# Four graph layers on one core: mixes by tiles, statistics ahead of evictions, and a few moved instructions

## The chip, the cores and the metric

The kernel runs on one core of one Trainium2 chip. The metric is the device time in microseconds (us), the median of three runs. A profiled execution of the same kernel gives the trace that is read here.

## The reference, cut to what matters

The input x holds 128 graphs of 64 nodes with 256 features each; adj is one 64 by 64 matrix for all graphs. Everything is in fp32. Each of four layers normalises x over its features, takes the positive part, runs its own network and adds the result to x.

```python
h = relu(layernorm(x)); x = x + L0(h)      # the same for L1, L2, L3
# L0: two graph convolutions, then LSTM windows of length 1 to 4 over the nodes
h = relu(einsum('ts,bsh->bth', adj, x @ Wg0 + bg0))
h = relu(einsum('ts,bsh->bth', adj, h @ Wg1 + bg1))
for p in 1..4: h[last node of each window of p] = lstm_last(Wih[p-1], Whh[p-1], windows of p)
# L1: masked attention with 4 heads
# L2: A_hat = normalised (adj + I)
h = relu(batchnorm(einsum('nm,bmd->bnd', A_hat, x) @ W1.T + b1)); out = batchnorm(h @ W2.T + b2)
# L3: weighting = adj * adj
h = relu(weighting . (x @ W1)); h = relu(weighting . (h @ W2)); out = weighting . (h @ W3)
```

## The kernel before, in words

The 8192 rows of x are cut into NG = 16 groups of 512 rows. A group is a tile of 128 partitions by GT = 4 row tiles by 256 features, so that a row tile holds two graphs. Most of x stays in SBUF from layer 1 on. Each layer runs over the groups, and the work of neighbouring groups overlaps.

**Mix.** A product with the 64 by 64 matrix of a layer is called a mix (the helper `mix`, matmuls on line 133). For each pair of column chunks it takes two PSUM banks and fills them with matmuls of 64 by 64: a loop over the two chunks c outermost, then over the four row tiles t, then over two column halves and the two graphs. In fp32 each of these matmuls is two instructions of TensorE, so that one pair of chunks is 64 instructions. Two copies then bring the banks to SBUF (lines 142, 145 and 381), one of them per graph, on the engines named in `copies`.

**Layer norm.** `ln_scale` takes statistics on VectorE (lines 90 and 92), adds epsilon (93), takes the power -1/2 on GpSimd (94) and multiplies on VectorE (96). `ln_apply` then runs one ScalarE activation for each row tile (101).

**Layer 0, convolutions.** The loop takes for each step `first_mix(g)`, `second_weights(g - 2)` (matmuls on 430), `second_mix` and `first_weights(g)` (matmuls on 406, an addition of `rb0` on VectorE in 414, a maximum on GpSimd in 415). The bias `rb0` is scaled by the row sums on line 346, behind group 1's place in VectorE's order. At group 4 the small forms of the adjacency are made, `normalized_adjacency` among them: 13 small VectorE instructions, one GpSimd power (326), a transpose on TensorE (280, four instructions), and a last product on VectorE (330). Its result `ah2` is used in layer 2 alone. The x of later groups is loaded into three buffers, and a load waits for the `ln_apply` that frees its buffer.

**Layer 0, LSTM, and layer 3's dense products** use a seven-product scheme for 2 by 2 blocks (helper `seven`): four products go first, then partial sums, then three more products, with the results added and finished by the callback `end`. The matmuls of the LSTM are on line 484, those of layer 3 on 1028, 1064 and 1109.

**Layer 1** is attention, with its projection weights in `w_att`. **Layer 2** makes `activated(g + 1)` and `mixed(g + 1)` ahead of `hidden(g)`. `hidden` runs sixteen matmul instructions (703) into four banks, and for each bank a ScalarE eviction with bias (709) and then VectorE statistics (712). The batch norm is finished after the last group (`bn_finish`), and a second loop runs the second weights (957). Its two weights come in one go at the end of layer 1, into a tile that follows `w_att`.

**Layer 3**: `start` (residual, layer norm, mix), `first_weights` (1028), `second_mix` (133, copies 142), `second_weights` (1064), `third_weights` (1109), `last_mix` (1130). In `first_weights` the last block (1, 0) of 128 by 512 is added on VectorE (176) and cut at zero on VectorE (204); the other blocks are cut on ScalarE (202, 206).

**Order.** Each engine runs its instructions in one fixed order, which the framework plans when the kernel is built: mostly as the program has it, but instructions that could start earlier are moved forward by the planner's costs. `tc.issue_after(ins)` puts the instructions of its block behind `ins` on the engine of `ins` only. Reading one PSUM bank from two engines is ordered too, in the order of the program. DMAs go out in the order of the issuing queue, here mostly that of SyncE (SP).

Of the kernel before, what the change touches and what calls it, by code (L numbers as in the profile page):

```python
# [10 lines left out]
ALU = mybir.AluOpType  # L11
# [3 lines left out]
P = 128  # L15
# [23 lines left out]
def adj_preln_kernel(ctx: ExitStack, tc: tile.TileContext, x_in, adj, vec, bg0, bg1,  # L39
# [42 lines left out]
    def ln_scale(src, between=None, n=GT):  # L82
# [10 lines left out]
        nc.vector.tensor_scalar(rstd, mv[:, :, 1], LN_EPS, None, ALU.add)  # L93
# [3 lines left out]
        return rstd, nmr, last.ins  # L97

    def ln_apply(src, dst, rstd, nmr, n=GT):
        for t in range(n):  # L100
            nc.scalar.activation(  # L101
                dst[:, t, :], src[:, t, :], AF.Relu,
                bias=nmr[:, t : t + 1], scale=rstd[:, t : t + 1],
            )

    def ln_relu(src, dst):

        rstd, nmr, _ = ln_scale(src)
        ln_apply(src, dst, rstd, nmr)
# [11 lines left out]
    def mix(src, a2, chunks, dst, copies, swap=False):  # L121
# [3 lines left out]
        for c0 in range(0, chunks, 2):  # L125
            pss = [bank((P, 2, GT, NODES)) for _ in range(2)]
            for c in range(2):
                for t in range(GT):
# [23 lines left out]
    def seven(products, banks, p1, p5, out, end):  # L152
# [14 lines left out]
        def finish():  # L167
# [8 lines left out]
            nc.vector.tensor_tensor(out[1][0], p1, ps[3], ALU.add)  # L176
            end(1, 0, None)
# [18 lines left out]
    def ends_in(out, func, on_vector=()):  # L196

        def end(m, n, ps):  # L200
            if ps is not None:
                nc.scalar.activation(out[m][n], ps, func)
            elif (m, n) in on_vector:
                nc.vector.tensor_scalar(out[m][n], out[m][n], 0.0, None, ALU.max)
            elif func != AF.Copy:
                nc.scalar.activation(out[m][n], out[m][n], func)  # L206

        return end
# [45 lines left out]
    with tc.tile_pool(name="lw", bufs=5) as lw:  # L254
# [6 lines left out]
        with tc.tile_pool(name="gw", bufs=1) as gw, tc.tile_pool(name="gcn", bufs=2) as gp, \  # L261
# [48 lines left out]
            def normalized_adjacency():  # L310
# [17 lines left out]
                pt2 = bank((P, NODES))  # L328
                by_batch(pt2, an)
                nc.vector.tensor_scalar(ah2, pt2, dinv, None, ALU.mult)  # L330
# [13 lines left out]
            with tc.issue_after(first_ln):  # L344
                nc.vector.tensor_reduce(rsum, arow, AX.X, ALU.add)
                nc.vector.tensor_scalar(rb0[:, 0, :], rb0[:, 0, :], rsum, None, ALU.mult)
# [4 lines left out]
            first_copied, first_scalar, middle_copied = None, None, None  # L351

            def first_mix(g):
                nonlocal first_copied, middle_copied, first_scalar
                h = gp.tile([P, GT, D], F32, tag="h", name="h")
                if g == 0:
                    for k, (rstd, nmr, _) in enumerate(lns):
                        two = slice(2 * k, 2 * k + 2)
                        ln_apply(xs[0][:, two], h[:, two], rstd, nmr, 2)
                elif g == 1:  # L360
                    with tc.issue_after(first_ln):
# [14 lines left out]
                if g == 0:  # L376
# [9 lines left out]
                    first_copied = copied  # L386
                else:
                    copied = mix(h, adj2, 2, m0, (on_vector, on_vector))
                if g == NG // 4:

                    with tc.issue_after(copied):
                        adjacency_forms()
                        normalized_adjacency()
                if g == NG // 2:
                    middle_copied = copied
                return m0
# [54 lines left out]
        with tc.tile_pool(name="back", bufs=1, reuse_waits="tile") as back_pool, \  # L451
# [22 lines left out]
            def gate_set(p, n, g, gates, w, bs):  # L474
# [25 lines left out]
                def end(m, blk, ps):  # L500
# [186 lines left out]
    def activated(pool, g):  # L687

        a = arena(pool)
        ln_relu(xs[g], a[:, 0:2, :].rearrange("p a (b d) -> p (a b) d", d=D))  # L690
# [6 lines left out]
    def hidden(g, w1, ms=range(4)):  # L697
        a = h1s[g]
        pss = []
# [8 lines left out]
        for m, ps in zip(ms, pss):  # L708
            nc.scalar.activation(
                a[:, m, :], ps, AF.Identity, bias=vecs[:, V_B1 + m : V_B1 + m + 1]  # L710
            )
            last = nc.vector.bn_stats(st1[:, m, g, :], ps)  # L712
        return last.ins


    with tc.tile_pool(name="att", bufs=2, reuse_waits="tile") as ap_:
# [113 lines left out]
        for g in range(NG + 1):  # L830
# [8 lines left out]
            if g == NG:  # L839

                w_l2 = weight_tile()
                w1 = w_l2[:, 0]
                w2 = w_l2[:, 1].rearrange("p (c f) -> p c f", c=4)
                w1 = w1.rearrange("p (c f) -> p c f", c=2)
                nc.sync.dma_start(out=w1, in_=w1t.rearrange("(c p) f -> p c f", p=P))
                nc.sync.dma_start(out=w2, in_=w2t.rearrange("(c p) f -> p c f", p=P))
# [3 lines left out]
            if g < NG:  # L850
                q, k = queries_keys(hT)
                v = ap_.tile([P, 2 * GT, P], F32, tag="v", name="v")
# [54 lines left out]
    behind = [after_attention, after_attention, counted]  # L907
    for g in range(1, NG):
        if g + 1 < NG:
            with tc.issue_after(behind[g - 1]):  # L910
                pool = ar_right if g + 1 < NG // 2 else keep if g + 1 == NG // 2 else ar_left
                activated(pool, g + 1)
                mixed(g + 1, (on_vector, on_vector))
# [336 lines left out]
```

## Time and profile before

| what | value |
|---|---|
| median of 3 runs | 2531.91 us (2531.35 to 2533.04) |
| profiled execution | 2532.12 us, its span 2530.3 us |
| TensorE busy | 2478.1 us, 98% of the span; mean granted clock 0.994 |
| VectorE, ScalarE, GpSimd busy | 1469.4, 1119.3, 419.4 us |
| chain that ended last | PE 90%, DVE 5%, ACT 2%, issue 1%, POOL 1%, DMA 1% |
| DMA | 39.64 MB, mean 16 GB/s |
| instruction fetch, queue 8 | 158 packets, 2.59 MB |

The span runs from the first to the last instruction; 1.8 us of the execution lie around it. In the profile PE is TensorE, PEld its weight loads, DVE VectorE, ACT ScalarE, POOL GpSimd and SP SyncE. A line of the timeline gives start, length, engine, line of the kernel, operation, tiles, shapes and count, and in brackets the idle time before it with what ended it. By the chain, the convolutions of layer 0 take the time up to 186 us, the LSTM up to 1232, attention up to about 1478, layer 2 up to about 1733, and layer 3 the rest.

### The profile page before, as it was taken

Reading aid. Unit: us, or ns where it says so; the run is one execution under the profiler, and the core shown is the slowest. Engines: PE = TensorE matmul, PEld = TensorE weight load, DVE = VectorE, ACT = ScalarE, POOL = GpSimd, SP = SyncE. Lnnn points to the kernel's source line nnn. Section 1 sums busy time; section 2 is a strip of 40 time slices with the busy share of each in tenths; the row PEclk is TensorE's granted clock in tenths of the full one; section 3 lists DMA queues with packets and bytes.
Section 4 is the critical chain, followed back from the end, with each engine's and each line's share of the span. In section 5 each row is a group of like instructions: output and inputs, shape, how many; then the busy total and the mean of one; then the engine's idle time right before and its main releaser. Section 6 shows DMA issues by size and latency. Waiting matters only on the chain.

```text
span 2530.3 us, 46856 instructions
## 1 busy us (share of the span) xinstructions
PE 2478.1 (98%) x20190; PEld 2044.8 (81%) x20190; DVE 1469.4 (58%) x2626; ACT 1119.3 (44%) x1967; POOL 419.4 (17%) x352
## 2 busy tenths in 40 slices
PE   6999999999999999999999999998999999999999
PEld 4668888889999998888766654445898888888888
DVE  5648876666566565565566666515455554554544
ACT  3547764444455343444455454653333332332332
POOL 3322211111111111111122221003111111111110
PEclk9999999999999999999999999998999999999999
DMA  3200000000000000000300000010000000000000
GB/s 112 102 2 1 1 17 1 1 1 34 1 1 1 1 1 1 1 13 1 101 2 2 2 19 1 1 48 12 9 10 10 18 10 9 18 10 9 18 9 18
DMA packets 30079, 39.64 MB, mean 16 GB/s; under 512 B 1584, under 2 KB 26288, under 8 KB 29872
## 3 DMA queue, kind: packets, MB, share of 16 engines
q1 hardware_dynamic: 29168, 36.09, 4.3%
q8 instruction: 158, 2.59, 0.4%
q10 hardware_dynamic: 704, 0.56, 0.1%
q14 instruction: 49, 0.40, 0.1%
HBM read 28.26 MB, written 8.39 MB: 14 GB/s over the span
## 4 chain that ended last, share of the span: by engine, by line
PE 90%; DVE 5%; ACT 2%; issue 1%; POOL 1%; DMA 1%; POOLq 0%; DVEq 0%; ACTq 0%
PE ps L484 40%; PE ps L1064 15%; PE ps L1109 8%; PE ps L731 4%; PE ps L957 4%; PE ps L1028 4%; PE ps L133 3%; PE ps L747 2%; PE ps L406 2%; PE ps L430 2%; DVE st L90 1%; POOL rstd L94 1%; PE ps L703 1%; ACT arena L101 1%; DVE st L712 1%
## 5 line engine op out<-in xcount | busy, mean ns | idle before, releaser
L484 PE MATMUL ps<-diff,s 128*128 128x256 f32 (+1 forms) x1824 | 393.5, 371 | 0.9 <-DVE diff L600 0.9
L1064 PE MATMUL ps<-arena 128*128 128x256 f32 x1792 | 392.6, 381 | 1.1 <-DVE arena L185 1.1
L1064 PEld LDWEIGHTS ps<-arena 128*128 128x128 f32 x1792 | 337.8, 190 | 55.3 <-issue 10.7
L484 PEld LDWEIGHTS ps<-diff,s 128*128 128x128 f32 x1824 | 345.9, 190 | 33.8 <-issue 1.6
L498 ACT ACTIVATE gates<-gates,lbias 128x512 f32<-128x512 f32 (+5 forms) x426 | 244.2, 621 | 203.6 <-DVE gates L173 146.5
L168 POOL TENSOR_TENSOR gates<-p 128x512 f32<-128x512 f32 (+1 forms) x115 | 148.6, 1292 | 882.8 <-DVE p L165 831.7
L484 PE MATMUL ps<-h,w 128*128 128x256 f32 (+1 forms) x1028 | 241.2, 371 | 1.6 <-ACT p L161 1.6
L484 PE MATMUL ps<-diff,w 128*128 128x256 f32 (+1 forms) x1040 | 238.7, 370 | 0.0
L484 PEld LDWEIGHTS ps<-diff,w 128*128 128x128 f32 x1040 | 197.4, 190 | 18.2
L484 PEld LDWEIGHTS ps<-h,w 128*128 128x128 f32 x1028 | 194.6, 190 | 20.9 <-ACT p L161 2.0
L498 ACT ACTIVATE gates<-ps,lbias 128x256 f32<-128x256 f32 (+3 forms) x213 | 91.7, 476 | 247.1 <-PE ps L484 247.0
L206 ACT ACTIVATE arena<-arena 128x512 f32<-128x512 f32 x128 | 78.7, 628 | 192.7 <-POOL arena L168 104.0
L168 POOL TENSOR_TENSOR arena<-arena 128x512 f32<-128x512 f32 x64 | 73.4, 1146 | 537.0 <-DVE arena L165 537.0
L1109 PE MATMUL ps<-arena 128*128 128x128 f32 x1280 | 149.9, 276 | 0.0
L1109 PEld LDWEIGHTS ps<-arena 128*128 128x128 f32 x1280 | 145.6, 192 | 1.3 <-issue 0.2
L173 DVE TENSOR_TENSOR gates<-p,ps 128x512 f32<-128x512 f32 (+1 forms) x115 | 76.4, 664 | 120.2 <-PE ps L484 120.2
L173 DVE TENSOR_TENSOR arena<-arena,ps 128x512 f32<-128x512 f32 x64 | 39.7, 621 | 149.1 <-PE ps L1064 84.3
L94 POOL TENSOR_TENSOR rstd<-rstd,mhalf 128x4 f32<-128x4 f32 (+1 forms) x66 | 66.7, 1010 | 338.5 <-DVE rstd L93 327.4
L703 PE MATMUL ps<-arena,w 128*128 128x512 f32 x256 | 115.2, 603 | 4.7 <-DVE arena L145 4.7
L484 PE MATMUL ps<-state,w 128*128 128x256 f32 (+1 forms) x512 | 116.1, 370 | 0.9 <-ACT p L161 0.8
L101 ACT ACTIVATE arena<-x,nmr,rstd 128x256 f32<-128x256 f32 x128 | 67.7, 590 | 109.8 <-DVE nmr L96 104.4
L484 PE MATMUL ps<-state,s 128*128 128x256 f32 (+1 forms) x512 | 115.8, 369 | 0.0
(186 smaller groups left out, 3934.5 us busy)
## 6 DMA issues: line engine op xcount, KB each, us to landing
x<-in_x SPq DMA_DIRECT2D x27, 512.0 KB, 7.6
out<-x SPq DMA_DIRECT2D x15, 512.0 KB, 2.9
w<-in_wih SPq DMA_DIRECT2D x4, 1024.0 KB, 7.3
w<-in_whh SPq DMA_DIRECT2D x3, 1024.0 KB, 6.2
arena<-in_l3w SPq DMA_DIRECT2D x3, 1024.0 KB, 5.2
w<-in_wqkv SPq DMA_DIRECT2D x1, 768.0 KB, 4.3
x<-in_x SPq DMA_DIRECT2D x2, 256.0 KB, 3.0
wg<-in_wg ACTq DMA_DIRECT2D x2, 256.0 KB, 7.2
```

Of the source, the lines that this page charges most:

```text
L94: nc.gpsimd.tensor_tensor(out=rstd, in0=rstd, in1=mhalf[:, 0:n], op=ALU.pow)
L101: nc.scalar.activation(dst[:, t, :], src[:, t, :], AF.Relu, bias=nmr[:, t : t + 1], scale=rstd[:, t : t + 1],)
L168: nc.gpsimd.tensor_tensor(out=out[1][1], in0=p1, in1=p5, op=ALU.add)
L173: nc.vector.tensor_tensor(out[0][1], p1, ps[1], ALU.add)
L484: nc.tensor.matmul(ps[:, r], lhsT=wc[:, j, :], rhs=bc, start=first and r == 0 and c == 0, stop=True, skip_group_check=True,)
L498: nc.scalar.activation(o, ps, func, bias=lbias[:, col : col + 1])
L703: nc.tensor.matmul(ps, lhsT=w1[:, c, m * P : (m + 1) * P], rhs=a[:, 2 + c, :], start=(c == 0), stop=(c == 1),)
L731: nc.tensor.matmul(ps, lhsT=wqk[:, c, col : col + P], rhs=hT[:, c, :], start=(c == 0), stop=(c == 1),)
L957: nc.tensor.matmul(pss[m], lhsT=w2[:, c, m * P : (m + 1) * P], rhs=a[:, c, :], start=(c == 0), stop=(c == 3),)
L1028: nc.tensor.matmul(ps[:, t, :], lhsT=w[:, t * P : (t + 1) * P], rhs=b, start=first and t == 0, stop=True, skip_group_check=True,)
L1064: nc.tensor.matmul(ps[:, r, :], lhsT=w[:, c, col : col + P], rhs=b[:, c, :], start=first and r == 0 and c == 0, stop=c == 1, skip_group_ch ...
L1109: nc.tensor.matmul(ps[:, t, :], lhsT=w[:, c, t * P : (t + 1) * P], rhs=b[:, c, :], start=first and t == 0 and c == 0, stop=c == 3, skip_gr ...
```

## The change

The changed kernel computes the same. It differs in these places:

- `mix` has the loop over row tiles t outermost and the one over chunks c inside it.
- In the first group of layers 0 and 3, the normalisation of row tile 3 moves from ScalarE (one instruction) to VectorE (two instructions). In layer 3's first group, the second half of the residual and its statistics come behind line 93 of the first half.
- The scaling of `rb0` and group 1's layer norm in layer 0 come behind the first group's copies on VectorE.
- The transpose on line 280 of the normalised adjacency and the product behind it come at group 8; the rest stays at group 4.
- In layer 2, statistics come ahead of evictions in the program; line 96 of group g + 1 comes behind the second statistics of group g - 2; one copy of each mix moves from VectorE to ScalarE.
- The first weights of layer 2 are loaded into the columns of `w_att` that the last queries and keys leave free, in the last step of attention; the second weights follow in two parts at group 3 of layer 2's loop in the program.
- Block (1, 0) of layer 3's first weights is added in two parts, one for each row tile, each cut at zero on ScalarE.

```diff
-        nc.vector.tensor_scalar(rstd, mv[:, :, 1], LN_EPS, None, ALU.add)
+        var = nc.vector.tensor_scalar(rstd, mv[:, :, 1], LN_EPS, None, ALU.add)
...
-        return rstd, nmr, last.ins
+        return rstd, nmr, (var if early else last).ins
...
+    def ln_apply(src, dst, rstd, nmr, n=GT, on_vector=()):
         for t in range(n):
+            if t in on_vector:
+                nc.vector.tensor_scalar(
+                    dst[:, t, :], src[:, t, :], rstd[:, t : t + 1], nmr[:, t : t + 1],
+                    ALU.mult, ALU.add,
+                )
+                nc.vector.tensor_scalar(dst[:, t, :], dst[:, t, :], 0.0, None, ALU.max)
+                continue
             nc.scalar.activation(
...
-            for c in range(2):
-                for t in range(GT):
+            for t in range(GT):
+                for c in range(2):
...
-            nc.vector.tensor_tensor(out[1][0], p1, ps[3], ALU.add)
-            end(1, 0, None)
+            for to, p, q in zip(*(parts(b) for b in (out[1][0], p1, ps[3]))):
+                nc.vector.tensor_tensor(to, p, q, ALU.add)
+                end(1, 0, None, to)
...
                 nc.vector.tensor_scalar(an, an, dinv, None, ALU.mult)
-                pt2 = bank((P, NODES))
-                by_batch(pt2, an)
-                nc.vector.tensor_scalar(ah2, pt2, dinv, None, ALU.mult)
+
+                def turned():
+                    pt2 = bank((P, NODES))
+                    by_batch(pt2, an)
+                    nc.vector.tensor_scalar(ah2, pt2, dinv, None, ALU.mult)
+
+                return turned
...
-                nc.vector.tensor_scalar(rb0[:, 0, :], rb0[:, 0, :], rsum, None, ALU.mult)
...
-                        ln_apply(xs[0][:, two], h[:, two], rstd, nmr, 2)
+                        ln_apply(xs[0][:, two], h[:, two], rstd, nmr, 2, (1,) if k else ())
                 elif g == 1:
-                    with tc.issue_after(first_ln):
+                    with tc.issue_after(first_copied):
                         rstd, nmr, _ = ln_scale(xs[1])
...
                     first_copied = copied
+                    with tc.issue_after(copied):
+                        nc.vector.tensor_scalar(rb0[:, 0, :], rb0[:, 0, :], rsum, None, ALU.mult)
...
                 if g == NG // 2:
                     middle_copied = copied
+                    turned()
...
         for m, ps in zip(ms, pss):
+            counted.append(nc.vector.bn_stats(st1[:, m, g, :], ps))
             nc.scalar.activation(
                 a[:, m, :], ps, AF.Identity, bias=vecs[:, V_B1 + m : V_B1 + m + 1]
             )
-            last = nc.vector.bn_stats(st1[:, m, g, :], ps)
...
+                if g == NG - 1:
+
+                    w1 = w_att[:, :, 0:512]
+                    w2 = w_att[:, :, 512:1024].rearrange("p a (b f) -> a p b f", f=D)
+                    nc.sync.dma_start(out=w1, in_=w1t.rearrange("(c p) f -> p c f", p=P))
...
-    behind = [after_attention, after_attention, counted]
+    behind = [[], [], counted]
     for g in range(1, NG):
         if g + 1 < NG:
-            with tc.issue_after(behind[g - 1]):
+            with tc.issue_after(behind[g - 1][-1].ins if behind[g - 1] else after_attention):
                 pool = ar_right if g + 1 < NG // 2 else keep if g + 1 == NG // 2 else ar_left
-                activated(pool, g + 1)
-                mixed(g + 1, (on_vector, on_vector))
+                activated(pool, g + 1, (lambda: behind[g][1]) if behind[g] else None)
+                mixed(g + 1, (on_scalar, on_vector))
+        if g == 3:
+            for a in range(2):
+                nc.sync.dma_start(
+                    out=w2[a], in_=w2t.rearrange("(a b p) f -> a p b f", a=2, p=P)[a]
+                )
         behind.append(hidden(g, w1))
...
-                to_residual(0, [k])
-                rstd, nmr, _ = ln_scale(xs[0][:, two], None, 2)
-                ln_apply(xs[0][:, two], h[:, two], rstd, nmr, 2)
+                with tc.issue_after(scaled) if k else nullcontext():
+                    to_residual(0, [k])
+                    rstd, nmr, scaled = ln_scale(xs[0][:, two], None, 2, True)
+                    ln_apply(xs[0][:, two], h[:, two], rstd, nmr, 2, (1,) if k else ())
...
-            blocks, ends_in(blocks, AF.Relu, [(1, 0)]),
+            blocks, ends_in(blocks, AF.Relu), lambda b: [b[:, t] for t in range(2)],
```

## The prediction, made before the changed kernel was run

> **What bounds the kernel now.** The page comes first: TensorE is busy for 98% of the span, so a gain can only come from the 52 us in which it is not, and from stretches at half clock.
>
> ```profile
> PE 2478.1 (98%) x20190; PEld 2044.8 (81%) x20190; DVE 1469.4 (58%) x2626; ACT 1119.3 (44%) x1967; POOL 419.4 (17%) x352
> ```
>
> TensorE's waits tell where these gaps lie (total us, times, longest).
>
> ```profile
> PE ps L280 <- DVE an L327: 5.8, 1, 5.8
> ...
> PE ps L406 <- ACT h L101: 4.7, 1, 4.7
> PE ps L703 <- DVE arena L145: 4.7, 7, 0.7
> PE ps L133 <- DVE arena L204: 4.6, 11, 0.4
> PE ps L133 <- ACT arena L101: 4.0, 1, 4.0
> ...
> PE ps L133 <- issue: 2.3, 1, 2.3
> ```
>
> They are the transpose of the normalised adjacency, layer 0's first weights, layer 2's hidden matmuls, layer 3's second mix, layer 3's first mix, and a stall at layer 2's entry. Next the timeline at each. In the first 65 us:
>
> ```profile
> 13.65 0.16 DVE L96 SCALAR_TENSOR_TENSOR nmr<-mv,rstd 128x4 f32<-128x4 f32 x1 [1.12 <-POOL rstd L94]
> 13.73 0.68 DVE L145 COPY m<-ps 128x512 f32<-128x512 f32 x1
> ...
> 14.51 6.29 PE L406 MATMUL ps<-wg,m 128*128 128x256 f32 x16 [4.71 <-ACT h L101]
> ...
> 58.05 0.48 PE L280 MATMUL ps<-ident,an 64*64 64x64 f32 x4 [5.81 <-DVE an L327]
> ...
> 58.46 6.52 PE L430 MATMUL ps<-m,wg 128*128 128x512 f32 x8
> ```
>
> The first mix ended at 9.80, but its copy stands behind line 96 of group 1, which waited for x, for GpSimd and behind a scaling. The transpose stops TensorE for 5.8 us, and the eight matmuls behind it take 6.52 us where the same eight take 3.70 at 32.52: half clock. In layer 2:
>
> ```profile
> 1540.64 0.70 DVE L712 BATCH_NORM_STATS2 st<-ps 128x6 f32<-128x512 f32 x1 [1.12 <-ACT arena L709]
> ...
> 1545.71 7.13 PE L703 MATMUL ps<-arena,w 128*128 128x512 f32 x16 [0.43 <-DVE arena L145]
> ...
> 1547.68 0.16 DVE L96 SCALAR_TENSOR_TENSOR nmr<-mv,rstd 128x4 f32<-128x4 f32 x1 [1.21 <-POOL rstd L94]
> ```
>
> VectorE, not TensorE, sets the pace: its statistics recur every 8.94 us (1533.26, 1542.19, 1551.13), whereas TensorE needs 8.16 (7.07 for the hidden matmuls, 1.09 for the mix). From 1500 to 1600 VectorE waits 22.3 us for line 709 and 13.3 for GpSimd. In layer 3:
>
> ```profile
> 2005.29 0.69 DVE L176 TENSOR_TENSOR arena<-arena,ps 128x512 f32<-128x512 f32 x1
> ...
> 2006.01 0.43 DVE L204 TENSOR_SCALAR arena<-arena 128x512 f32<-128x512 f32 x1
> ...
> 2006.49 1.86 PE L133 MATMUL ps<-w2s,arena 64*64 64x64 f32 x112 [0.41 <-DVE arena L204]
> ```
>
> After 16 of 128 instructions the mix waits for the last block's sum and cut.
>
> [...] The page's 158 fetches of 2.59 MB are 16 KB each.
>
> **The change part by part.** The sum is made against the profiled execution, 2532.12 us (2530.3 span and 1.8 around it), 0.2 above the median of 2531.91.
>
> *Layer 0, first groups.* Line 101 takes about 0.5 us a tile; three tiles stay on ScalarE, from 6.32 to 7.9. Tile 3 costs VectorE two instructions, 0.41 and 0.42 (lines 983 and 204, nearest rows), from 6.7 to 7.5: ahead of ScalarE's third. The mix by tiles then ends near 9.0 (9.80 before), and its copy of 0.68, with nothing ahead of it, near 9.7. Line 406 starts there, not at 14.5: 4.8 us. What was passed is late next: the scaling of `rb0` (0.35, its DMA lands at 10.6), then group 1's norm: 1.4 for four statistics, 0.5 for lines 92 and 93, 1.0 for GpSimd, 0.2, and 2.1 on ScalarE, ending near 16.3. TensorE is covered until then by line 406, 16 matmuls at 0.43 cold, to 16.5. The next weights (26.09) waited 2.0 us for copies that stood behind such a line 96, the mix ahead 0.7 for GpSimd, and their half clock cost 1.7 (loads of 5.01 against 3.32 us). Following the chain (mix to 17.6, GpSimd's second 1.49 to 18.7, second mix to 19.4) the next weights start near 19.5: 6.6 us earlier, with the clock 8.3. No load of x is late: group 4's had landed by 19, later ones follow the pipeline. Bounds 4 to 10.
>
> *Transpose.* At group 4 the 13 small instructions and a power (54.8 to 57.9) still run on VectorE, but only line 435 queues behind them; its banks are wanted an iteration (9.5 us) later. So 5.8 goes, and with it 2.8 of half clock: 8.6. At group 8 `an` is long done; the four matmuls (0.48) and line 330 (0.28) only move. Bounds 5 to 9.
>
> *Entry of layer 2.* TensorE stalls 2.3 us in the middle of a mix, waiting for no semaphore, while both weight loads run (issued 1477.16 and 1477.58, landing 1480.87 and 1482.48); then eight matmuls take 4.86, not 3.60. I read this as an instruction fetch behind 1 MB of weights. The first load leaves SP about 5 us earlier, when queries and keys are done. The second is placed later in the program, but SP has nothing between, so it may go out when the values are done, near 1477, as before, in two issues. Half the traffic stays: I take 1.5, bounds 0 and 3.6.
>
> *Layer 2's loop.* VectorE's waits for line 709 go, the power (1.2) is covered by two statistics, and one copy (0.65) goes to ScalarE. By busy time over count VectorE then has 4 x 0.67 + 4 x 0.36 + 0.72 + 0.65 = 5.5 us a group and ScalarE 4 x 0.53 + 4 x 0.63 + 0.57 = 5.2, both under 8.16. TensorE's waits of 4.7 go; I take 4.5, bounds 0 and 5.5. The added wait of line 96 holds the norm of g + 1 until hidden(g - 2), with a mix and a hidden (8 us) in between; that covers statistics, line 96 and ScalarE's 2.1. Evictions start 0.7 later, but a bank is free as soon as before.
>
> *End of layer 2's first pass.* The last statistics no longer follow a 0.67 eviction: 0.7, bounds 0 and 1.5.
>
> *Layer 3's first mix.* The first half's line 93 comes a residual add (0.68) earlier. The mix ends 16 instead of 40 cold instructions after the last tile, some 0.7: 1.6 with the tile on VectorE, bounds 0 and 2.5.
>
> *Layer 3's second mix, 16 times.* The sum of 0.69 becomes two of 0.42 (line 176 at 256 columns). ScalarE cuts (0, 1) until 2006.06, then the halves by about 2006.45 and 2006.8 (0.38 each, line 202 at 256 columns). TensorE has 32 instructions ahead of tile 2 rather than 16 and would finish the first pair of chunks at 2007.1, not 2007.27: 0.2 a group, 3.2 in all. ScalarE's order decides; bounds -1 (cuts behind another ScalarE instruction) and 6 (all waits gone).
>
> Layer 0's other mixes, the attention and the LSTM have the same instructions, and only the order within a mix changes there: nothing, since TensorE has no wait for their inputs.
>
> Sum: 8.3 + 8.6 + 1.5 + 4.5 + 0.7 + 1.6 + 3.2 = 28.4, so 2503.7 for the profiled execution, 2503 for the median. All lower bounds leave 8 us of gain, all upper ones 38.
>
> **The rivals.** *The start-up gives back half.* Group 1's norm starts later, and if it or GpSimd's maxima come several us after line 406, TensorE idles there and stays cold. For it: the norm is ready only 0.2 us ahead. Against it: VectorE is about half busy there. It gains 20: 2512.
>
> *Layer 2 stays bound by VectorE or banks.* For it: each bank is still read twice in turn. Against it: 5.5 of 8.16 us. No gain in layer 2 at all: 22, so 2510.
>
> *Applies behind evictions: slower.* If the planner leaves line 101 of group g + 2 behind ScalarE's evictions of hidden(g), its mix waits after hidden(g)'s end for a statistic 0.69, an eviction 0.67 and a first tile 0.59, and then runs at ScalarE's pace: about 2.6 us for each of 14 groups, 36. The other parts give 24 (28.4 - 4.5): 2544. It decides from 24/14 = 1.7 us a group. For it: the added wait and the copy sit on that engine. Against it: in the trace the planner has moved line 101 between evictions.
>
> *The change doesn't do what it says.* The planner leaves the copy and the transpose where they stood: what remains is 2 to 5 us, within the bound of no change.
>
> **How the numbers follow.** My forecast 0.62; the start-up rival 0.14; layer 2 bound 0.12; no effect 0.03; slower 0.09. About 0.2% (5 us) is what a measurement can tell from no change, so faster 0.88, same 0.03, slower 0.09. The range takes the forecast's own bounds and the first two rivals: 2494 (upper bounds, 38) to 2521 (lower bounds of most parts, 11); the rest is left out.
>
> **What would show it.** Right: line 280 behind line 133 at group 8 without a wait; line 406 starting near 10; layer 2's statistics every 8.2 us with no wait for line 709; line 133 in layer 3 waiting under 0.3 us in two pieces; no "issue" stall near 1470. Wrong: TensorE waiting for line 101 in layer 2, for line 415 or 101 before 40 us, or a second half-clock stretch before 60 us.

## The result, and the profile after

| what | before | after |
|---|---|---|
| median of 5 runs | 2531.77 us (2528.84 to 2533.04) | 2508.33 us (2507.45 to 2509.02) |
| ratio after to before | | 0.9908, 95% interval 0.9894 to 0.9923 |
| span of the profiled execution | 2530.3 us | 2506.7 us |
| mean granted clock | 0.994 | 0.996 |

The change saves 23.4 us of the medians and 23.6 us of the spans. The forecast was 28.4 and 2503 us, with a range from 2494 to 2521; the sign and the range held, and one term of the sum was far too large. Beside the later experiments the kernel before took 2527.5 to 2528.6 us (medians), so that end times of those runs can be set against 2508.33 only to within 3 or 4 us.

The engines' line of the page after:

```profile
PE 2473.8 (99%) x20190; PEld 2044.8 (82%) x20190; DVE 1458.3 (58%) x2616; ACT 1137.7 (45%) x2011; POOL 419.1 (17%) x352
```

TensorE is now idle for 33 us of the span instead of 52. Its waits over the whole span (total us, times, longest):

```profile
PE ps L287 <- DMA arow<-in_adj: 5.5, 2, 4.0
PE ps L141 <- ACT arena L109: 4.2, 3, 2.8
...
PE ps L141 <- ACT h L109: 1.9, 2, 1.0
...
PE ps L419 <- DVE m L153: 1.3, 1, 1.3
...
PE ps L141 <- issue: 1.0, 1, 1.0
...
PE ps L419 <- ACT m L391: 0.9, 1, 0.9
```

Lines have moved: the mix is 141 (133 before), its copies are 153 and 150 (145, 142), the apply is 109 (101) with 103 and 107 on VectorE, layer 0's first weights are 419 (406) with 427 and 428 behind them (414, 415), its second weights 443 (430), the transpose 287 (280), layer 2's hidden matmuls 716 (703) with statistics 722 (712) and evictions 723 (709), and layer 3's second weights 1083 (1064). Three of the six waits that the prediction showed are gone: 5.8 us for the transpose, 4.7 for the copies into the arena (the tiles of intermediate results) in layer 2, and 4.6 for line 204. Those for line 101 in layer 0 and for the "issue" at layer 2's entry have shrunk; the one in layer 3's first mix has changed its shape only.

The two spans can be set against each other at the same TensorE instruction. Down to layer 3's loop, every row is how much less time lies between two such instructions in the second trace:

| stage | forecast, us | measured, us |
|---|---|---|
| start of layer 0, until about 47 us | 8.3 | 3.2 |
| transpose, with its half clock | 8.6 | 9.1 |
| LSTM and attention | 0 | 0 |
| entry of layer 2 | 1.5 | 2.0 |
| layer 2's loop | 4.5 | 5.2 |
| end of layer 2's first pass | 0.7 | -0.2 |
| layer 3's first mix | 1.6 | 1.0 |
| layer 3's loop | 3.2 | 3.5 |
| behind the last matmul | 0 | -0.1 |
| sum, of the exact values | 28.4 | 23.6 |

Now the start of layer 0, where the forecast is missed by 5 us. The timeline of after, from the first copies to the second first weights:

```profile
9.62 0.69 DVE L153 COPY m<-ps 128x512 f32<-128x512 f32 x1 [2.05 <-PE ps L141]
...
10.41 6.71 PE L419 MATMUL ps<-wg,m 128*128 128x256 f32 x16 [0.89 <-ACT m L391]
...
11.80 0.36 DVE L92 BATCH_NORM_AGGREGATE mv<-st 128x2 f32<-128x6 f32 x4
12.81 0.43 DVE L90 BATCH_NORM_STATS2 st<-x 128x6 f32<-128x256 f32 x1 [0.65 <-DMA x<-in_x]
14.20 0.69 DVE L427 TENSOR_TENSOR h<-ps,rb 128x512 f32<-128x512 f32 x1 [0.96 <-PE ps L419]
14.80 0.16 DVE L93 TENSOR_SCALAR rstd<-mv 128x4 f32<-128x4 f32 x1
...
14.97 1.50 POOL L428 TENSOR_SCALAR h<-h 128x512 f32<-128x512 f32 x1 [8.41 <-DVE rstd L93]
16.44 1.04 POOL L94 TENSOR_TENSOR rstd<-rstd,mhalf 128x4 f32<-128x4 f32 x1
...
18.36 3.85 PE L141 MATMUL ps<-adj,h 64*64 64x64 f32 x128 [0.88 <-ACT h L109]
...
23.49 3.81 PE L419 MATMUL ps<-wg,m 128*128 128x256 f32 x9 [1.28 <-DVE m L153]
```

The first copy does start with nothing ahead of it, and the first weights at 10.41. But group 1's norm, whose means (line 92) are there at 12.16, goes on with line 93 only at 14.80: VectorE's fixed order has a statistic of group 2 in between, which waits for a DMA, and then line 427, which waits for TensorE. On GpSimd the same addition's maximum (428) then stands for 1.5 us ahead of the power (94). The next mix starts at 18.36 and the next weights, which wait for a copy, at 23.49, still at half clock: 3.81 us for nine matmuls, where sixteen take 3.72 at full clock (shown in the first experiment).

In layer 2 the timeline of one period:

```profile
1562.50 0.70 DVE L722 BATCH_NORM_STATS2 st<-ps 128x6 f32<-128x512 f32 x1 [1.02 <-PE ps L716]
...
1563.48 7.13 PE L716 MATMUL ps<-arena,w 128*128 128x512 f32 x16
...
1565.27 0.16 DVE L93 TENSOR_SCALAR rstd<-mv 128x4 f32<-128x4 f32 x1
1565.50 0.70 DVE L722 BATCH_NORM_STATS2 st<-ps 128x6 f32<-128x512 f32 x1
...
1567.22 0.70 DVE L722 BATCH_NORM_STATS2 st<-ps 128x6 f32<-128x512 f32 x1 [1.02 <-PE ps L716]
1567.84 0.14 DVE L96 SCALAR_TENSOR_TENSOR nmr<-mv,rstd 128x4 f32<-128x4 f32 x1
...
1570.65 0.70 DVE L722 BATCH_NORM_STATS2 st<-ps 128x6 f32<-128x512 f32 x1 [1.02 <-PE ps L716]
```

The statistics recur every 8.15 us and wait for TensorE, not TensorE for VectorE; the hidden matmuls have no bracket at all. Two statistics stand between lines 93 and 96, where before VectorE waited 1.21 us for GpSimd. The prediction's 8.94 us was VectorE's pace before, not yet TensorE's: VectorE's fourth statistic of a group came every 8.94 us from group 1 on, but TensorE kept its 8.16 until VectorE was far enough behind, and behind the entry only seven of its periods were longer (8.66 once, 8.94 six times), with the seven waits of line 703 that the prediction lists. That is the whole 5.2 us of the table.

In layer 3 the timeline of one second mix:

```profile
1984.09 0.75 DVE L185 TENSOR_TENSOR arena<-arena,ps 128x256 f32<-128x256 f32 x2
1984.47 2.45 PE L141 MATMUL ps<-w2s,arena 64*64 64x64 f32 x128
```

All 128 instructions run in one piece of 2.45 us; before there were 16, a wait of 0.41 us, and 112.

### The profile page after: what moved, and what is told of

Same layout as the page of the kernel before. It is cut to its first block, busy times and chain, and to the rows that moved or that the text cites. A ratio compares the mean times of both kernels' runs of the same rounds, so it can differ in the third digit from the quotient of the medians.

```text
span 2506.7 us, 46889 instructions
## 1 busy us (share of the span) xinstructions
PE 2473.8 (99%) x20190; PEld 2044.8 (82%) x20190; DVE 1458.3 (58%) x2616; ACT 1137.7 (45%) x2011; POOL 419.1 (17%) x352
## 4 chain that ended last, share of the span: by engine, by line
PE 93%; DVE 3%; ACT 1%; POOL 1%; issue 1%; DMA 0%; DVEq 0%; ACTq 0%; POOLq 0%
PE ps L497 40%; PE ps L1083 15%; PE ps L1128 8%; PE ps L744 4%; PE ps L975 4%; PE ps L716 4%; PE ps L141 4%; PE ps L1047 3%; PE ps L419 2%; PE ps L760 2%; PE ps L443 2%; PE ps L821 1%; PE ps L124 1%; ACT arena L213 1%; PE ps L246 1%
## 5 line engine op out<-in xcount | busy, mean ns | idle before, releaser
L213 ACT ACTIVATE arena<-arena 128x512 f32<-128x512 f32 (+1 forms) x160 | 88.6, 582 | 192.4 <-POOL arena L176 103.6
L181 DVE TENSOR_TENSOR gates<-p,ps 128x512 f32<-128x512 f32 (+1 forms) x115 | 76.5, 665 | 119.7 <-PE ps L497 119.7
L185 DVE TENSOR_TENSOR gates<-p,ps 128x512 f32<-128x512 f32 (+1 forms) x115 | 76.8, 668 | 64.6 <-PE ps L497 63.9
```

Source lines behind the costliest of these rows:

```text
L181: nc.vector.tensor_tensor(out[0][1], p1, ps[1], ALU.add)
L185: nc.vector.tensor_tensor(to, p, q, ALU.add)
L213: nc.scalar.activation(o, o, func)
```

## The experiments

Each run is compared with after by stages, between the same two TensorE instructions, since end times that differ by 3 to 4 us for one and the same kernel before are too coarse for some of the questions. With the same code ahead of them the first weights of layer 0 begin anywhere between 9.6 and 11.6 us, and with the same code at layer 3's start its half clock lasts 10.2 or 13.7 us. For a single run the end time is given beside the stage. Line numbers differ by a few between these kernels, since an edit shifts them.

### Group 1's norm ahead of the later norms and the first additions on VectorE

`ln1` is group 1's scale, made right behind the scaling of `rb0`; the norms of groups 2 and later and the additions of the first weights come behind it.

```diff
-                    with tc.issue_after(first_copied):
-                        rstd, nmr, _ = ln_scale(xs[1])
+                    rstd, nmr, _ = ln1
...
-                    with tc.issue_after(first_copied):
+                    with tc.issue_after(ln1[2]):
                         ln_relu(x, h)
...
+                    with tc.issue_after(ln1[2]):
                         nc.vector.tensor_tensor(hk, ps, rb0.to_broadcast([P, 2, D]), ALU.add)
```

> The changed kernel, with group 1's layer norm made ahead of the first sums of layer 0 on VectorE, and the norms of later groups behind it. Theory (the order on VectorE and GpSimd cost the start-up 5 us: line 93 of group 1 stood behind a statistic of group 2 that waited for its x, and behind a sum that waited for TensorE): line 96 of group 1 ends near 13.8 instead of 17.7, the second run of first weights starts by 20.5 instead of 23.5, and the kernel gains 3 to 5 us over the changed one, near 2504. Rival (the start is bound by the half clock from 19.9 to 26.8 or by landing times): the norm is earlier but the kernel gains less than 1 us.

Measured: 2505.41 us, median of five (2504.87 to 2507.26), ratio to before 0.9913 (0.9899 to 0.9926). The timeline of this kernel:

```profile
11.87 0.36 DVE L92 BATCH_NORM_AGGREGATE mv<-st 128x2 f32<-128x6 f32 x4
12.26 0.17 DVE L93 TENSOR_SCALAR rstd<-mv 128x4 f32<-128x4 f32 x1
12.51 1.01 POOL L94 TENSOR_TENSOR rstd<-rstd,mhalf 128x4 f32<-128x4 f32 x1 [6.01 <-DVE rstd L93]
13.55 0.16 DVE L96 SCALAR_TENSOR_TENSOR nmr<-mv,rstd 128x4 f32<-128x4 f32 x1 [1.12 <-POOL rstd L94]
...
20.21 3.72 PE L419 MATMUL ps<-wg,m 128*128 128x256 f32 x16 [0.50 <-DVE m L153]
...
36.87 3.70 PE L444 MATMUL ps<-m,wg 128*128 128x512 f32 x8 [1.22 <-ACT m L153]
...
41.60 0.69 PE L141 MATMUL ps<-adj,h 64*64 64x64 f32 x32 [0.41 <-POOL h L429]
```

The norm runs through from 11.87 to 13.71, the second first weights start at 20.21 instead of 23.49, and so the order on VectorE and GpSimd cost these 3.3 us there: from the first weights to the second it now takes 9.7 us, where the prediction had 9.8 and after took 13.1. But of the 3.3 us only 2.0 are left when the LSTM starts, counted from the first weights (158.6 against 160.6 us): between 31 and 52 us the two waits shown, 1.22 and 0.41, come up where after has none. That all sixteen matmuls run at full clock here is not this edit's doing: the kernel of a later experiment, with both copies of layer 2 on VectorE, has after's code at the start, and its timeline shows full clock too:

```profile
23.29 3.72 PE L419 MATMUL ps<-wg,m 128*128 128x256 f32 x16 [2.26 <-DVE m L153]
...
34.47 1.78 PE L419 MATMUL ps<-wg,m 128*128 128x256 f32 x7 [1.64 <-DVE m L153]
```

Its third first weights start at 34.47, after's, with the half clock, at 34.55 without a wait. TensorE waits longer where it runs faster; the half clock costs nothing there. The expected 3 to 5 us didn't come. Against their own runs of before, this kernel saves 22.6 us and after 23.4, and the two ratios can't be told apart; the 2.0 us are a reading of the stage.

### The start as before

The diff puts the scaling of `rb0`, group 1's norm and tile 3's apply back where they were; the rest of the change stays.

```diff
+                nc.vector.tensor_scalar(rb0[:, 0, :], rb0[:, 0, :], rsum, None, ALU.mult)
...
-                        ln_apply(xs[0][:, two], h[:, two], rstd, nmr, 2, (1,) if k else ())
+                        ln_apply(xs[0][:, two], h[:, two], rstd, nmr, 2)
...
-                    with tc.issue_after(first_copied):
+                    with tc.issue_after(first_ln):
```

> The changed kernel with the scaling of rb0, group 1's norm and the first group's norm on ScalarE as they were before. Theory (the start-up edits give 3.2 us, the transpose the other 9.1 before 66 us): 3 us slower than the changed kernel, with the same start of layer 0's second first weights as before (26.1), and still no wait at the transpose. Rival (the two share their gain, since both shorten one stretch of half clock): 0 to 1 us, or over 5.

Measured: 2510.57 us, one run. TensorE's waits of this kernel show the old one again:

```profile
PE ps L418 <- ACT h L109: 4.5, 1, 4.5
```

The first weights start at 14.05 us, the second at 25.27 (expected 26.1), and the LSTM at 173.70, 2.7 us later than in after. In the eight profiles with after's start and tiles outermost the LSTM starts between 170.6 and 172.4 us, so the start-up part of the change is worth some 1 to 3 us: the two traces' 3.2 lies at the upper end, and 8 is out of the question. No wait at the transpose comes back, so the two parts don't share their gain.

### The transpose back at group 4

```diff
-                        turned = normalized_adjacency()
+                        normalized_adjacency()()
...
-                    turned()
```

> The changed kernel with the transpose and its product back at group 4. Theory (5.8 us of wait and 2.8 of half clock behind it): 8 to 9.5 us slower than the changed kernel, the eight matmuls behind the transpose at 6.5 us. Rival (the earlier start has moved the small instructions, so that the wait is mostly covered): under 4 us.

Measured: 2515.48 us, one run. The timeline of this kernel:

```profile
54.19 0.48 PE L287 MATMUL ps<-ident,an 64*64 64x64 f32 x4 [4.88 <-DVE an L334]
54.60 6.49 PE L442 MATMUL ps<-m,wg 128*128 128x512 f32 x8
```

The wait of 4.9 us is back, and with it the half clock: eight matmuls in 6.49 us for 3.70. From the first weights of group 3 to those of group 4 it takes 17.6 us, in after 9.5. The transpose is thus worth 8.2 us with the new start, within the expected 8 to 9.5, and 9.1 against before, where its wait was 0.9 us longer. It is the largest part of the gain, and it is shown alone. The end time rose by 7.2 only; this profile has 1.2 us less at layer 3's start, where its half clock is 10.2 us long.

### Layer 3: chunks outermost, and the last block in one piece

```diff
-            for t in range(GT):
-                for c in range(2):
+            for c in range(2):
+                for t in range(GT):
```

> The changed kernel with the chunks outermost in every mix, as before. Theory (order by tiles gives TensorE twice the work ahead of a late tile, 0.28 us at tile 2 and more at tile 3): layer 3's group takes 48.0 to 48.1 us against 47.6 in the changed kernel and 47.84 before, so that the cuts by parts on ScalarE are a loss without it; 6 to 8 us slower in all. Rival (the cuts by parts give the gain, the order nothing): layer 3's group stays within 0.1 of 47.6, 0 to 1 us slower.

Measured: 2514.1 us, one run. And tiles outermost, with block (1, 0) whole, but still cut on ScalarE:

```diff
-            blocks, ends_in(blocks, AF.Relu), lambda b: [b[:, t] for t in range(2)],
+            blocks, ends_in(blocks, AF.Relu),
```

> The changed kernel with block (1, 0) of layer 3's first weights added whole and cut whole on ScalarE. Theory (parts hide the second sum behind the first cut): the block is ready about 0.4 us later, layer 3's group takes 47.9 to 48.0 us against 47.6, 5 us slower in all. Rival (ScalarE is held by the cut of block (0, 1) anyhow, so parts give nothing): under 1 us slower.

Measured: 2511.3 us, one run. TensorE's waits from 1780 to 2490 us, for the kernel with chunks outermost:

```profile
PE ps L141 <- ACT arena L213: 3.7, 11, 0.3
```

and for the kernel with the block whole:

```profile
PE ps L141 <- ACT arena L213: 4.2, 11, 0.4
```

In after there is none in this stretch. Layer 3's period, in its last ten groups, is 47.84 us before, 47.95 with chunks outermost, 47.81 with the block whole, 47.60 after. Put in parts for one alone: the order by tiles, with a whole cut on ScalarE, is worth 0.03 us, parts with the old order cost 0.11, and both together save 0.24. I read this so: the second part of the block must be needed late for the split to pay, and the first part must be ready early for the order to pay. In both kernels the block is cut on ScalarE, before on VectorE; no run has one of the two edits with the cut on VectorE, so what the move of the cut does by itself is open. In the second to fourth period, where last mixes and transposes of other groups run between, it is 49.19 us before and 48.94 to 48.95 in all three others: there either edit is enough, or the cut on ScalarE that all three share.

The first expectation (48.0 to 48.1) was some 0.1 us too high, the second lay between what theory and rival gave; by the end times, chunks outermost is 5.8 us slower than after (expected 6 to 8) and the whole block 3.0 (expected 5). Chunks outermost also take 0.95 us more at the start of layer 3, and 1.2 more from layer 0's first weights to the LSTM (0.8 against the other kernels with after's start).

### Layer 2: which of three edits sets the period

Four kernels undo the edits of layer 2's loop, first one at a time, then two together.

```diff
-            counted.append(nc.vector.bn_stats(st1[:, m, g, :], ps))
             nc.scalar.activation(...)
+            counted.append(nc.vector.bn_stats(st1[:, m, g, :], ps))
```

> The changed kernel with layer 2's evictions ahead of the statistics again. Theory (VectorE's wait for each eviction made it the bound): the loop's period is 8.4 to 8.9 us against 8.16, 3 to 5 us slower. Rival (the copy moved to ScalarE and the statistics in the power's wait are enough): the period stays 8.16 and the time within 0.5 us.

```diff
-                mixed(g + 1, (on_scalar, on_vector))
+                mixed(g + 1, (on_vector, on_vector))
```

> The changed kernel with both copies of layer 2's mixes on VectorE. Theory (VectorE then has 6.1 us of work a group, under TensorE's 8.16): no change, within 0.5 us. Rival (VectorE with its waits is still near the bound): period above 8.3, over 1.5 us slower.

```diff
-                activated(pool, g + 1, (lambda: behind[g][1]) if behind[g] else None)
+                activated(pool, g + 1)
```

> The changed kernel without the added place of line 96 in layer 2 (it follows the power directly). Theory (VectorE waits 1.2 us more a group, 6.7 us in all, under 8.16): no change, within 0.5 us. Rival (the wait pushes the statistics back and holds the banks): over 1.5 us slower.

And the first two of these together:

> Two of layer 2's edits are undone together: the evictions stand ahead of the statistics, and both copies of the mix are on VectorE. The new place of line 96 and everything else stay. Theory: each of the edits takes enough off VectorE's chain to let TensorE set the period, so that one alone could be undone without loss, and two undone together make VectorE late again: the period of the layer-2 loop rises from 8.16 us to between 8.4 and 8.9 us, with waits of TensorE for the arena's copies of 0.2 to 0.8 us in a group, and the loop of some seven groups takes 2 to 5 us more. Rival: the place of line 96, or that the mixes take tiles outermost, is enough alone: the period stays within 0.05 us of 8.16 us, and no wait for the arena's copies is over 0.1 us.

Measured: 2509.05, 2507.91, 2508.36 and 2508.45 us, one run each, and in all four a period of 8.16 us with no wait of TensorE for the arena's copies. So the second and third went as theory had it, and for the first and the fourth the rival held. VectorE's timeline in the fourth, taken from the view of all engines:

```profile
1567.47 0.17 DVE L93 TENSOR_SCALAR rstd<-mv 128x4 f32<-128x4 f32 x1
1567.55 0.69 DVE L725 BATCH_NORM_STATS2 st<-ps 128x6 f32<-128x512 f32 x1
...
1568.53 0.70 DVE L725 BATCH_NORM_STATS2 st<-ps 128x6 f32<-128x512 f32 x1 [0.30 <-ACT arena L722]
1569.15 0.14 DVE L96 SCALAR_TENSOR_TENSOR nmr<-mv,rstd 128x4 f32<-128x4 f32 x1
```

The evictions are first, so a statistic waits 0.30 us for ScalarE, and both copies are on VectorE. Yet line 96 has no bracket, because two statistics cover GpSimd's power. The same place before the change, in VectorE's timeline of that kernel:

```profile
1573.11 0.17 DVE L93 TENSOR_SCALAR rstd<-mv 128x4 f32<-128x4 f32 x1
1574.50 0.16 DVE L96 SCALAR_TENSOR_TENSOR nmr<-mv,rstd 128x4 f32<-128x4 f32 x1 [1.21 <-POOL rstd L94]
1574.58 0.69 DVE L712 BATCH_NORM_STATS2 st<-ps 128x6 f32<-128x512 f32 x1
1576.39 0.70 DVE L712 BATCH_NORM_STATS2 st<-ps 128x6 f32<-128x512 f32 x1 [1.12 <-ACT arena L709]
1577.94 1.29 DVE L712 BATCH_NORM_STATS2 st<-ps 128x6 f32<-128x512 f32 x2 [0.85 <-ACT arena L709]
```

Waits of 1.21, 1.12 and 0.85 us follow each other on one engine, each engine's turn behind the other's. With line 96 in its new place and the mixes by tiles, the old order of evictions and copies is fast enough; and without line 96's place (third kernel), statistics first and one copy on ScalarE are fast enough. What is left open is whether line 96 alone, with chunks outermost, would do: the kernel with chunks outermost has all three of the other edits and also 8.16 us. Evictions or copies alone, with line 96 in its old place, weren't run either.

That TensorE's period is the same in all four doesn't mean that the edits do nothing. VectorE's own pace shows where it has fallen behind at the entry and catches up. Its fourth statistic of a group came every 8.94 us before. With evictions and copies in their old places it comes every 7.88 us, six times in a row, until it has caught up; with evictions alone in their old place, every 7.3 us, twice (and twice in the last kernel below). So the place of line 96, with the order by tiles, took about 1.06 us off VectorE's chain, and moving the copy another 0.6. The edits add up; TensorE's 8.16 us hides all that goes beyond the first 0.78.

Statistics ahead of evictions are not free either. From 1500 to 1600 us the evictions in after wait for statistics 37 times, 39.5 us in all, where before the statistics waited 22.3 us for evictions. With the evictions first, the entry of layer 2 takes 0.9 us less (21.78 against 22.69 us for the first two groups' matmuls; the 0.6 us that a mix of after waits there for line 109 don't come up), and the phase of the second weights 113.25 instead of 113.53 us. In the fourth kernel and in the last one below, both with evictions first, the entry takes 0.7 us less.

### Layer 2's weights

First, the second weights issued on ScalarE behind the evictions of group 3, so that they can't go out with the attention's last values:

```diff
+            with tc.issue_after(evicted[-1].ins):
                 for a in range(2):
-                    nc.sync.dma_start(
+                    nc.scalar.dma_start(
```

> The changed kernel with the second weights of layer 2 loaded from ScalarE's queue behind the last eviction of group 3, so that no load runs at the entry of layer 2. Theory (the stall of TensorE there is an instruction fetch that waits behind the weights in the DMA rings): the stall of 1.0 us waiting for no semaphore goes, the fetch starts before 1467 and not as the weights end, about 1 us faster than the changed kernel. Rival (four blocks of small matmuls in a row outrun the fetch whatever the loads do): the stall stays at 0.8 us or more.

Then both loads where they were before the change:

> The changed kernel with both weight loads of layer 2 as before, together after the attention's last values. Theory (twice the bytes ahead of the fetch): the stall is 2.3 us again and the half clock behind it comes back, 1.5 to 3 us slower than the changed kernel. Rival (the stall differs by chance): it stays near 1 us.

Measured: 2506.63 and 2510.11 us, one run each. TensorE's timeline at the entry, with the loads as before:

```profile
1471.76 0.62 PE L141 MATMUL ps<-ah,arena 64*64 64x64 f32 x19 [2.40 <-issue]
1472.31 5.29 PE L716 MATMUL ps<-arena,w 128*128 128x512 f32 x8
```

and in after:

```profile
1470.58 0.56 PE L141 MATMUL ps<-ah,arena 64*64 64x64 f32 x19 [0.96 <-issue]
1471.07 3.70 PE L716 MATMUL ps<-arena,w 128*128 128x512 f32 x8
```

and with the second weights later:

```profile
1469.95 0.56 PE L141 MATMUL ps<-ah,arena 64*64 64x64 f32 x19 [0.73 <-issue]
```

The old place costs 2.2 us: a stall of 2.40 instead of 0.96 us, and half clock behind it (5.29 us for eight matmuls instead of 3.70). In after both parts of the second weights do go out with the values (1464.74 and 1465.20), and a packet of the instruction queue (queue 8) starts at 1468.07, just after the last weight packet ends at 1467.89; before, the packet started at 1481.72 and the weights ended at 1481.82. But in after the weights don't hold the packet back. With the second weights later, the weight packets end at 1462.5 and the packet starts at 1467.63; counted from attention's last matmul of keys and queries (line 779 in after) that is 0.35 us, in after 0.40, and 1.67 and 1.68 with the loads in the old place (before and the second kernel here).

The eleven kernels with after's loads stall for 0.80 to 1.39 us, the one without a load 0.73, the two with the old loads 2.33 and 2.40: the rival of chance doesn't hold for the old place, and 0.73 us of stall is left without any load. Of the first kernel's expectation neither the end of the stall nor a start of the fetch before 1467 came, nor the whole microsecond: the entry of two groups takes 22.69 us in both, and the same in six other kernels with stalls up to 1.39 us.

### The two best edits together

The kernel after the change, with group 1's norm ahead and evictions first in layer 2:

> The kernel after the change with two edits from the earlier runs together: at the start, the scale of group 1's first normalisation stands ahead of group 2's statistics and adds on VectorE and GpSimd; in layer 2 the evictions stand ahead of the statistics, as before the change. Theory: the parts add, since they lie in different stages: 2.0 us at the start (fw0 to the recurrence's start) and 1.2 us in layer 2 (0.9 us at its entry, 0.3 us in its second weights), so 3 us under the kernel after the change: 2505 us, 2503.5 to 2507, against 2508.3. Rival: the stages move against each other and one of the parts is given back to a wait for ScalarE: 2506 to 2508 us, with only one of the two stage times shorter.

Measured: 2503.99 us, median of four (2502.78 to 2505.45), ratio to before 0.990 (0.9882 to 0.9918). By stages against after: from the first weights to the LSTM 158.3 for 160.6 us (161.0 in seven other kernels with after's start), layer 2's entry 21.94 for 22.69, its second weights 113.24 for 113.53. That is 3.3 us, against an expected 3; a further 1.1 at layer 3's start (half clock of 10.2 instead of 13.7 us) and a loss of 1.2 in the first loads are not the edits'. It has the lowest median of all the kernels run, but against its own runs of before it saves 24.6 us where after saves 23.4, and the intervals of the ratios overlap, so that it beats after is shown by the stages only.

## Why the prediction was right or wrong

The total alone would have misled: 2508.3 us lies nearer to the totals of two rivals (2510 and 2512) than to the forecast of 2503. Only the stages tell which terms held.

**Start of layer 0: the step that failed.** It was forecast at 8.3 us and brought 3.2. The prediction had the first weights at 9.7 and group 1's norm ready near 16.3 by adding 1.4, 0.5, 1.0, 0.2 and 2.1 us behind the scaling of `rb0`. The sum of durations was right: in the first experiment the chain takes 5.28 us, from 10.55 to 15.83, and in after 9.31, from 10.48 to 19.79. What failed is that it took the chain as running without a stop. `issue_after(first_copied)` puts the instructions behind the copies and says nothing of what may come between them; group 2's statistic and line 427 did, and cost 2.6 us on VectorE and then 1.5 on GpSimd. So the next weights came 2.6 us earlier instead of 6.6. The chain without the stop isn't the whole of it: the first experiment has it, and still gains only 2.0 of the missing 5.1 us by the LSTM. The term of 1.7 for the half clock failed for another reason: TensorE waits for VectorE's copies there, and a kernel with after's start at full clock is no further on (third first weights at 34.47 against 34.55). What the rest of the miss consists of is open. The measured 3.2 lies below the lower bound of 4, which did not allow for a foreign instruction within the chain. It is the mechanism of the rival "the start-up gives back half", group 1's norm coming some us after line 406, and it took 5.1 us where that rival's total lay 8.4 under the forecast's.

**Transpose: right.** 9.1 for 8.6, and 8.2 when it is undone alone. In the trace of before TensorE stands still for 5.81 us until 58.05, and a stretch of half clock runs from 57.33 to 64.16; in that of after neither is there (granted clock 1.00 from 40 to 100 us), and the eight matmuls behind the transpose went from 6.5 to 3.7 us. With the transpose back at group 4 they take 6.49 us again.

**Entry of layer 2: the number right, the account only in part.** 2.0 for 1.5. The reading that weights and an instruction fetch meet there is supported by the two experiments (2.40, 0.96, 0.73 us of stall), and so is the remark that the second weights may go out with the values, as they did. The prediction kept part of the stall because half of the traffic stays; the runs show that this traffic delays nothing there, and that what is left of the stall comes without it too. That the packet of queue 8 holds the very instructions that TensorE lacked is an inference, but a close one: in all fourteen profiles the stall comes at the same matmul in TensorE's order, within one, and ends 1.4 to 1.6 us after that packet.

**Layer 2's loop: right, and more than was needed.** 5.2 for 4.5, with the period down from 8.94 to the 8.16 that the prediction took for TensorE's need. It added the waits for line 709, the power and the copy as if each edit took off its share, and VectorE's pace (8.94, 7.88, 7.3 us) says that line 96 and the copy do. But 0.78 us a group was all that TensorE could gain, so that none of the three is needed when the other two stand, and without the first two it still holds. "Bound by VectorE" was a chain of waits between three engines, not VectorE's 34 us of work in 53.

**End of layer 2's first pass: sign wrong.** Forecast 0.7, measured -0.2. The last statistics there don't wait for an eviction only: each stands in VectorE's order behind the finishing of the block before, about 2.6 us a block (line 906, GpSimd's 0.54, three small products), against 1.7 of TensorE. That the phase of the second weights is 0.28 us faster with evictions first fits: the order of statistics ahead of evictions costs here what was booked as a gain. The lower bound of 0 excluded this without a reason.

**Layer 3.** The first mix brought 1.0 for 1.6: its first half starts earlier, but then the mix waits again, 0.78 us, for the second half, which is now behind line 93 of the first. No run undoes these two edits alone. The loop brought 3.5 for 3.2; the halves were cut one behind the other as the working had it, and the short waits in two pieces that it allowed for didn't come. The two experiments show that in the last ten groups order and split are both needed.

**The other rivals** did not come true. In layer 2 neither VectorE nor the banks stayed the bound. As for the slower one, line 109 has three of its tiles between the evictions of the group before (1568.54), and no mix of the loop waits for it.

## What to carry to other kernels

An instruction put behind another in an engine's order is not put directly behind it: before counting on a chain, look at what the engine may take up between its links, above all a statistic that waits for a load or an addition that waits for TensorE (here 2.6 us on VectorE). Where an engine seems to set the pace at 60% busy, look for a ring of waits between engines; here one place (with the order by tiles) took 1.06 us off a ring that was 0.78 us too slow, and the further cures bought nothing, or cost elsewhere. Splitting a block and reordering its consumer can be worth next to nothing alone (here a gain of 0.03 us a group and a loss of 0.11) and something together (0.24). And an order that one engine is late in can stay hidden for groups on end, until the slack between the engines is used up (here VectorE came every 8.94 us a group, TensorE every 8.16 but for seven periods).

## What the runs showed of the hardware

In these fourteen profiles the half clock comes in pieces: they list stretches of 3.4, 6.8, 10.2 and 13.7 us, which are one to four times 3.41, apart from the last one of each run. Before has 3.41, 6.83, 3.41 and 13.65 us and at the end 3.78, after has 6.83, 13.65 and at the end 3.87. With the same code, layer 3's start had three such pieces in the profiles of five kernels and four in those of six, among them after, and the stage from its first transposes to its first second weights took 24.1 to 24.5 us in the first and 25.0 to 25.6 in the second. And TensorE stalled on "issue" in the middle of a mix for 0.73 us in the one kernel in which no weight load was running there, for 0.80 to 1.39 us in the eleven in which the loads ended just before the packet of instructions, and for 2.33 and 2.40 us in the two in which the packet started only as the loads ended.
